# The feed-forward of the last token tile, moved into the first tiles of the next stage

## The chip, the cores and the metric

The kernel runs on one core of a Trainium2 chip. The metric is the device time of one execution in microseconds (us), taken as the median of several runs. A core has five engines that work side by side, each with an instruction queue of its own that it takes in order: TensorE (PE, matrix products, with its weight loads shown apart as PEld), VectorE (DVE), ScalarE (ACT, activation functions and copies), GpSimd (POOL) and SyncE (SP, which here issues most DMA transfers). Engines wait for one another by semaphores.

## The reference

The reference is a stack of eight residual blocks on an activation `x` of 2 sequences by 1024 tokens by 256 channels, in float32. Each block adds its output on the layernorm of `x`. Two of them follow each other at the place of the change, and a third comes after:

```
x = x + L1_attn_a(layernorm(x))   # differential attention
x = x + L1_ffn(layernorm(x))      # feed-forward
x = x + L1_attn_b(layernorm(x))   # trained linear model
x = x + L1_ffn(layernorm(x))      # the same feed-forward
```

The feed-forward works on each token by itself, with `Wg`, `Wu` and `Wd` unpacked from 4-bit codes:

```
gate = x @ Wg.T                   # 256 -> 2048
up = x @ Wu.T                     # 256 -> 2048
inter = gelu_tanh(gate) * up
out = inter @ Wd.T                # 2048 -> 256
```

The trained linear model runs through the tokens in chunks of 16, in order. For each chunk it applies a state `S` (16 by 16 for each of 16 heads) to the keys, normalizes the result, makes from it a correction `v_new`, and subtracts the product of keys and `v_new` from `S`; the queries see the state from before the chunk and the chunk's own earlier tokens. So each chunk needs the state that the chunk before left:

```
kh = ki @ S ; v_new = f(normalized kh, vi - ki)
qh = qi @ S - A @ v_new ; o = qi + ln(qh)
S = S - (ki * ei).T @ v_new
```

## The kernel before

`x` lies in on-chip memory (SBUF) for the whole run, as 16 slabs of 128 tokens. A token tile `i` (0 to 7) is slab `i` of both sequences, 256 tokens in all. A stage works through the eight tiles. Stages are set up by `build`, which runs the first four blocks, unpacks the feed-forward's weights into `deq`, and then calls `attn_d_ffn1` (differential attention and the first use of the last feed-forward) and `ttt_ffn1` (linear model and its second use).

**`attn_d_ffn1`** writes the order of its work out by hand. The attention of a tile is 16 units, and the loop runs one number `n` for each unit, with the parts of neighbouring units interleaved. Other steps are hung on a number by `add(n, step)`: those of tile `i` on the numbers of the tile after it, so that they fill gaps between attention units. They are the attention's output (`squares`, `root`, `normalize`, `project` from `attn_d_out`; the projection is L1181, its addition to `x` L1187) and then the feed-forward from `ffn1_parts`: layernorm (`stats`, `rows`, `turn`), eight gate pieces (L1255, each copied out of the one accumulator buffer `ph` by ACT at L1261), one gelu over everything (L1266), eight up pieces (L1255 again, multiplied in by DVE at L1263) and eight down pieces (L1272, added to `x` at L1279). After the last tile no attention is left to be interleaved with, and the loop runs on over the numbers that still have steps. The attention's own matmul of weights and values is `py` (L1122).

**`ttt_ffn1`** first scales the linear model's weights on DVE (`ln_w`, `ln_b`, the value part of `wt` at L1348, `wto` at L1350), which `build` loads just before through SP (L104: `wt`, `wto`, `wbeta`, `wg`) and ACT (L114: `ln_w`, `ln_b`; L1824: three small ones). These weights lie in a pool `w1`, set up after the attention's weight pool `wd` has been released (`wd_.release()`), so they take over its memory and their loads wait for its last use.

Then `ttt_inputs(0)` prepares tile 0: layernorm, transposition, projection to query, key and value, transposes of keys and queries by head, products of keys and queries (`pa`, L1416), learning rates and gates. Keys also take a way through DRAM (`uk_d`), from which they come back as `r`. The main loop then runs 8 tiles by 8 steps `n`, a step being two chunks of 16 tokens (one of each sequence). In a step PE applies the state to the queries (`pq`) and to the keys of the next step (`kh`, with a correction for the chunk just done), and makes the state's change `ds`; all these are lines L1416, 32 by 32 products in groups of 16 calls. DVE adds `ds` to `S` (L1393) and does the normalization and correction in small instructions (`ttt_step`). After these, each step runs the pieces of a list `fill[n]`: parts of the preparation of the next tile (`inputs`), of the output of the tile before (`outputs`), and of the second feed-forward of earlier tiles from `ffn1_tile`. That is cut into 14 pieces: 0 rows (layernorm), 1 turn, 2 to 9 the eight hidden chunks (gate and up into `pg` and `pu`, L1733, 16 matmul calls; gelu on ACT L1738; multiply on DVE L1739), 10 to 13 the four down pieces (L1746; the addition to `x` is L1753). A tile's pieces 0 to 4 are run in the steps 4, 6 and 7 of the tile after it (`ffn`), pieces 5 to 13 in the tile after that (`last_ffn`). In tiles 0 and 1 `last_ffn` holds empty pieces, and in tile 0 `ffn` as well. PE's order in this stage is that of the program; for the other engines a scheduler decides.

The lists that decide where a piece runs:

```
fill = [
    [outputs[0], inputs[0], *last_ffn[5:7], inputs[1]],
    [last_ffn[7], inputs[2]],
    [*last_ffn[8:10], inputs[3]],
    [last_ffn[10], inputs[7], outputs[1]],
    [last_ffn[11], outputs[2], ffn[0], inputs[4]],
    [last_ffn[12], inputs[8], inputs[5], inputs[6]],
    [last_ffn[13], ffn[1], ffn[2]],
    [ffn[3], ffn[4]],
]
```

Of the kernel before, what the change touches and what calls it, by code (L numbers as in the profile page):

```python
# [23 lines left out]
NB = T // P  # L24
# [20 lines left out]
class Net:  # L45
# [772 lines left out]
    def attn_d_ffn1(self, w, wo, cos, sin, nlam, rms_w, deq):  # L818

        nc, tc = self.nc, self.tc
        NH, NKV, D = 16, 4, 16
        with ExitStack() as ctx:
            big = ctx.enter_context(tc.tile_pool(name="d_big", bufs=1))
            work = ctx.enter_context(tc.tile_pool(name="d_work", bufs=2))
            ps = ctx.enter_context(tc.tile_pool(name="d_ps", bufs=1, space=PSUM))
            self.ps = tc.alloc_tile_pool(name="d_ps0", bufs=1, space=PSUM)  # L830
            self.small = True

            nc.vector.tensor_scalar(
                wo, wo, rms_w, 1.0 - (0.8 - 0.6 * math.exp(0.0)), ALU.mult, ALU.mult
            )

            in_g = big.tile([P, 4], F32, name="in_g")
            nc.gpsimd.memset(in_g, 1.0)
            for pattern, base, cm in (([[-32, 4]], 0, 1), ([[32, 4]], 15, -1)):
                nc.gpsimd.affine_select(  # L840
                    out=in_g, in_=in_g, compare_op=ALU.is_ge, fill=0.0, base=base,
                    pattern=pattern, channel_multiplier=cm,
                )
            half = big.tile([P, 2], F32, name="half")
            nc.vector.tensor_reduce(half[:, 0:1], in_g, AX.X, ALU.add)
            nc.vector.tensor_scalar(half[:, 1:2], half[:, 0:1], -1.0, 1.0, ALU.mult, ALU.add)

            mask = big.tile([P, T], BF16, name="mask")
            nc.gpsimd.memset(mask[:, 0 : T - P], 0.0)
            nc.gpsimd.tensor_copy(mask[:, T - P : T], self.neg)  # L850
            ctx.enter_context(self.in_order())

            kT = [big.tile([P, 2, T], F32, name=f"kT{b}") for b in range(B)]
            v = [big.tile([P, NB, NKV, 32], F32, name=f"v{b}") for b in range(B)]
            for b in range(B):
                nc.gpsimd.memset(v[b][:, :, :, D:32], 1.0)
            pools = (ps, work, w, cos, sin, half, nlam, mask)
            at, pairs = {}, []  # L860

            def add(n, *steps):
                at.setdefault(max(n, -1), []).extend(steps)

            for i in range(NB):
                n = 16 * i
                tile_ = type("tile", (), {})()
                blocks = [
                    self.attn_d_block(pools, tile_, b, i, kT[b], v[b]) for b in range(B)
                ]  # L870
                for m, step in zip(
                    (-9, -8, -6, -4, -4, -2, -2, -2, -1, -1, -1, -1, -1),
                    (*self.attn_d_inputs(ps, work, tile_, i), *blocks[0][0], *blocks[1][0]),
                ):
                    add(n + m if i else -1, step)
                for _, units in blocks:
                    pairs.extend(units)

                n += 16
                squares, root, normalize, project = self.attn_d_out(ps, work, tile_, wo, i)  # L880
                stats, rows, turn, gate, gelu, up, down = self.ffn1_parts(ps, work, i, deq)
                for m, step in (
                    (2, squares), (3, root), (4, normalize), (5, project), (5, stats), (6, rows),
                    (7, turn), *((8 + k // 2, gate[k]) for k in range(8)), (11, gelu),
                    *((13 + k // 2, up[k]) for k in range(8)),
                    *((17 + k // 2, down[k]) for k in range(8)),
                ):
                    add(n + m, step)
            nothing = type("nothing", (), {"large": False})()

            def pair(n):
                return pairs[n] if 0 <= n < len(pairs) else nothing

            def do(u, name, *args):
                f = getattr(u, name, None)
                if f:
                    f(*args)

            for step in at[-1]:
                step()  # L900
            for n in range(max(at) + 1):
                if n == 16 * 4:

                    self.ps.release()
                    self.ps = tc.alloc_tile_pool(name="d_ps1", bufs=1, space=PSUM)
                    self.small = False
                fill = at.get(n, [])
                k = (len(fill) + 2) // 3, (2 * len(fill) + 2) // 3
                u, last, turned, weighed = (pair(n - j) for j in range(4))
                do(u, "scores", 0)  # L910
                do(u, "highest", 0)
                if not u.large:
                    do(u, "exponentials")
                do(weighed, "weigh")
                do(last, "ratio")
                for step in fill[: k[0]]:
                    step()
                do(turned, "turn", 0)
                if u.large:
                    u.scores(1)  # L920
                    u.highest(1)
                for step in fill[k[0] : k[1]]:
                    step()
                do(turned, "turn", 1)
                if u.large:
                    u.exponentials()
                do(last, "difference")
                for step in fill[k[1] :]:
                    step()
            self.ps.release()  # L930
# [358 lines left out]
    def ttt_ffn1(self, w, deq):  # L1289
# [5 lines left out]

        nc, tc = self.nc, self.tc
        D = 16
        with ExitStack() as ctx:  # L1300
# [56 lines left out]
            nc.vector.memset(t.S, 0.0)  # L1357
            ctx.enter_context(tc.manual_schedule(engines={mybir.EngineType.PE}))
            data, inputs = self.ttt_inputs(0)
            for piece in inputs:  # L1360
                piece()
            vs = self.ttt_step(0, data, None)
            outputs = ffn = last_ffn = [lambda: None] * 20
            for i in range(NB):
                next_data, inputs = None, [lambda: None] * 9
                if i + 1 < NB:
                    next_data, inputs = self.ttt_inputs(i + 1)
                fill = [
# [36 lines left out]
                last_ffn, ffn = ffn, self.ffn1_tile(i, deq)  # L1405
# [357 lines left out]
def build(tc, ins, out, first=0, last=6):  # L1763
    nc = tc.nc
    with ExitStack() as ctx:
# [2 lines left out]
        net.make_constants()  # L1768
        nlam = net.diff_lambda(ins)
        todo = STAGES[first:last]  # L1770
        wd_ = tc.alloc_tile_pool(name="wd", bufs=1)
        p = "L1_attn_a_"
        wd = net.load_w(wd_, "wd", [ins[p + k] for k in ("Wq", "Wk", "Wv")])
        wdo = net.load_w(wd_, "wdo", [ins[p + "Wo_ugtd"]])
# [3 lines left out]
        with tc.tile_pool(name="w0", bufs=1) as w0:  # L1778
# [21 lines left out]
            if {"attn_d", "ttt"} & set(todo):  # L1800
                w4 = ctx.enter_context(tc.tile_pool(name="w4", bufs=1, side="right"))
                deq = [
                    net.dequantize(w4, k, ins[f"L1_ffn_{k}_packed"], ins[f"L1_ffn_{k}_scales"])
                    for k in ("gate", "up", "down")
                ]
        if "attn_d" in todo:
            net.attn_d_ffn1(wd, wdo, *rope_d, nlam, rms_w, deq)
        wd_.release()
        if "ttt" in todo:
            w1_ = ctx.enter_context(tc.tile_pool(name="w1", bufs=1))  # L1810
            p = "L1_attn_b_"
# [80 lines left out]
def program(arrays, first=0, last=6):  # L1892
    import concourse.bacc as bacc

    nc = bacc.Bacc("TRN2", target_bir_lowering=False, num_devices=1)
    ins = {
        k: nc.dram_tensor(f"in_{k}", v.shape, mybir.dt.from_np(v.dtype), kind="ExternalInput").ap()
        for k, v in arrays.items()
    }
    out = nc.dram_tensor("out", (B, T, C), F32, kind="ExternalOutput").ap()  # L1900
    with tile.TileContext(nc) as tc:
        build(tc, ins, out, first, last)
    return nc
# [9 lines left out]
```

## Time and profile before

| What | Value |
|---|---|
| Median of 3 runs | 3162.74 us (3157.12 to 3170.88) |
| The profiled execution | 3170.71 us, its span 3168.9 us |
| PE busy | 2640.7 us (83%) |
| DVE busy | 1922.1 us (61%) |
| ACT busy | 1355.2 us (43%) |
| POOL busy | 1030.5 us (33%) |
| Mean granted PE clock | 0.89 |

The page divides the span into 40 slices of 79 us. The first 29 hold roughly the blocks up to the differential attention, the last 11 the last tile's feed-forward and the linear model. The durations below are of the one profiled execution. Times of a view are counted from the start of its span. "PEclk" is the share of the full PE clock that was granted in a stretch; it is read beside each duration of a matmul, because the same matmul takes longer at a lower clock. A busy time of PE includes matmuls that run slowly, and an engine that is idle costs time only where others wait for it.

### The profile page before, as it was taken

To read this page: it belongs to the slowest core of one execution; us is meant where nothing else is said; L and a number is where in the kernel's file an instruction comes from. 1 tells how busy PE (TensorE), PEld (TensorE's weight loads), DVE (VectorE), ACT (ScalarE), POOL (GpSimd) and SP (SyncE) were. 2 spreads that over 40 slices of the span, in tenths; PEclk is the share of its full clock that TensorE was granted. 3 is DMA by queue.
4 is the path that set the end of the run, shared out by engine and by line. 5 is a ranking of instruction groups with operands and counts; after the bars stand their busy time and mean duration, and the time that the engine had idled before them with its cause. 6 is when DMAs were issued, how large, how long until landed. Compare 5 with 4: busy or idle time off the path is not lost.

```text
span 3168.9 us, 66877 instructions
## 1 busy us (share of the span) xinstructions
PE 2640.7 (83%) x26384; PEld 1622.8 (51%) x26384; DVE 1922.1 (61%) x6646; ACT 1355.2 (43%) x2713; POOL 1030.5 (33%) x1648
## 2 busy tenths in 40 slices
PE   6888889699997866978887878878867689889998
PEld 2233245343433433655655555555644567767777
DVE  4776650576765446666676867778615665665652
ACT  2785942144454334664655555656512121221210
POOL 2444210211203456566564655656500000000000
PEclk8999989799998975988989888898987699999999
DMA  3000000000001100000000000000001111001000
GB/s 111 1 1 1 1 1 0 1 1 1 1 1 27 47 8 1 1 1 1 1 1 1 1 1 1 1 1 1 1 18 22 30 23 22 10 22 36 22 10 14
DMA packets 61978, 35.38 MB, mean 11 GB/s; under 512 B 43216, under 2 KB 58080, under 8 KB 61664
## 3 DMA queue, kind: packets, MB, share of 16 engines
q1 hardware_dynamic: 59472, 29.49, 3.6%
q8 instruction: 208, 3.41, 0.4%
q10 hardware_dynamic: 2192, 1.61, 0.2%
q14 instruction: 106, 0.87, 0.1%
HBM read 22.68 MB, written 8.39 MB: 10 GB/s over the span
## 4 chain that ended last, share of the span: by engine, by line
PE 36%; DVE 13%; ACT 7%; issue 4%; POOL 3%; DMA 0%; POOLq 0%; DVEq 0%; ACTq 0%; SPq 0%
PE ph L1255 6%; PE po L1746 4%; DVE p L1057 4%; PE e L1046 4%; ACT p L1068 4%; PE pg L1733 4%; PE pu L1733 3%; PE dT L1105 3%; PE po L1272 2%; POOL p L1081 2%; DVE p L1094 2%; PE py L1122 1%; PE pa L1416 1%; PE kh L1416 1%; PE pq L1416 1%
## 5 line engine op out<-in xcount | busy, mean ns | idle before, releaser
L1057 DVE CUSTOM_DVE_ANT_0 p<-e,mask 128x512 f32<-128x512 f32 (+3 forms) x768 | 381.7, 553 | 106.4 <-PE e L1046 105.1
L1068 ACT ACTIVATE p<-p,nm 128x128 f32<-128x128 f32 (+7 forms) x512 | 389.9, 764 | 97.7 <-DVE nm L1057 88.1
L1081 POOL TENSOR_SCALAR p<-p,ra,neg_lam 128x128 f32<-128x128 f32 (+7 forms) x256 | 222.8, 870 | 235.6 <-DVE ra L1077 180.9
L1105 PE MATMUL dT<-ident,p 128*128 128x128 f32 x1152 | 200.5, 308 | 112.9 <-ACT pT L1109 29.7
L1109 ACT ACTIVATE pT<-dT 128x128 f32<-128x128 f32 (+7 forms) x256 | 165.5, 647 | 285.8 <-PE dT L1105 284.5
L1046 PE MATMUL e<-kT,qT 32*128 32x512 f32 (+3 forms) x1536 | 234.2, 625 | 28.0 <-DVE nm L1057 26.7
L196 POOL TENSOR_SCALAR ln_mv<-ln_mv 128x2 f32<-128x2 f32 x48 | 15.7, 328 | 739.9 <-DVE ln_mv L194 728.3
L1094 DVE CUSTOM_DVE_ANT_0 p<-p,rs 128x128 f32<-128x128 f32 (+7 forms) x256 | 207.8, 833 | 69.8 <-POOL p L1085 69.6
L1105 PEld LDWEIGHTS dT<-ident,p 128*128 128x128 f32 x1152 | 154.7, 158 | 173.2 <-POOL p L1085 49.5
L723 ACT ACTIVATE pr<-s 128x512 f32<-128x512 f32 (+3 forms) x384 | 157.1, 496 | 167.6 <-PE s L718 164.4
L1098 POOL TENSOR_SCALAR p<-p,md 128x128 f32<-128x128 f32 (+7 forms) x256 | 208.2, 813 | 25.4
L437 ACT ACTIVATE pr<-s 128x1024 f32<-128x1024 f32 (+1 forms) x192 | 146.1, 821 | 126.7 <-PE s L431 123.1
L1255 PE MATMUL ph<-xT,up 128*128 128x256 f32 x512 | 138.2, 419 | 20.0 <-DVE inter L1263 18.3
L683 PE MATMUL s<-kT,qT 32*128 32x512 f32 (+3 forms) x768 | 151.2, 531 | 2.3 <-ACT pr L723 1.3
L442 ACT ACTIVATE pr<-pr 128x1024 f32<-128x1024 f32 (+1 forms) x192 | 153.0, 861 | 0.0
L1255 PE MATMUL ph<-xT,gate 128*128 128x256 f32 x512 | 138.5, 417 | 15.8 <-ACT xT L225 10.8
L691 DVE CUSTOM_DVE_ANT_0 masked<-s,mask 128x128 f32<-128x128 f32 (+3 forms) x256 | 110.7, 487 | 55.0 <-PE s L683 54.6
L1746 PE MATMUL po<-down,inter 128*128 128x256 f32 x512 | 140.7, 437 | 2.2 <-DVE x L1753 1.2
L445 POOL TENSOR_SCALAR_AFFINE_SELECT pr<-pr 128x256 f32<-128x256 f32 x128 | 93.5, 747 | 146.0 <-ACT pr L442 84.4
L1733 PE MATMUL pg<-xT,gate 128*128 128x256 f32 x512 | 131.3, 401 | 7.5 <-ACT xT L225 5.5
L456 PE MATMUL py<-pr,v 128*32 128x512 f32 (+3 forms) x768 | 115.1, 541 | 26.6 <-POOL pr L445 24.6
L1255 PEld LDWEIGHTS ph<-xT,up 128*128 128x128 f32 x512 | 101.2, 207 | 62.3 <-DVE inter L1263 28.9
(301 smaller groups left out, 5440.1 us busy)
## 6 DMA issues: line engine op xcount, KB each, us to landing
uk_d<-uk SPq DMA_DIRECT2D x128, 32.0 KB, 1.8
r<-uk_d SPq DMA_DIRECT2D x8, 512.0 KB, 4.2
x<-in_L_attn_a_X SPq DMA_DIRECT2D x4, 512.0 KB, 6.1
qh_d<-qh SPq DMA_DIRECT2D x8, 256.0 KB, 2.7
o<-qh_d SPq DMA_DIRECT2D x128, 16.0 KB, 1.8
out<-x SPq DMA_DIRECT2D x4, 512.0 KB, 3.1
w<-in_L_ffn_W2T SPq DMA_DIRECT2D x1, 1024.0 KB, 7.9
pk<-in_L_ffn_gate_packed SPq DMA_DIRECT2D x8, 128.0 KB, 2.4
```

The costliest lines, as they stand in the source:

```text
L723: nc.scalar.activation(pr[:, g, off:512], tiles[g][:, 0:m], AF.Exp, scale=0.25)
L1046: nc.tensor.matmul(own.tiles[h][:, a, 0 : hi - lo], made["q"][r : r + 32, a, t, :], kT[r : r + 32, a, lo:hi], start=True, stop=True,)
L1057: nc.vector.tensor_tensor_reduce(own.p[h][a][:, lo:hi], own.tiles[h][:, a, 0 : hi - lo], neg_row[:, T - nk + lo : T - nk + hi], -1.0, 3e38 ...
L1068: nc.scalar.activation(own.p[h][a], own.p[h][a], AF.Exp, bias=own.nm[:, h, a : a + 1], scale=-1.0, accum_out=own.sm[:, h, a : a + 1],)
L1081: nc.gpsimd.tensor_scalar(p1, p1, own.ra[:, h : h + 1], nlam[:, head : head + 1], ALU.mult, ALU.mult)
L1094: nc.vector.tensor_tensor_reduce(p0, p0, p1, own.rs[:, h, 0:1], -3e38, ALU.add, ALU.max, md)
L1098: nc.gpsimd.tensor_scalar(p0, p0, md, 1.0, ALU.add, ALU.mult)
L1105: nc.tensor.transpose(dT[:, kb, :], own.p[h][0][:, kb * P : (kb + 1) * P], self.ident)
L1109: nc.scalar.activation(pT[:, 0 : qb + 1, :], dT[:, 0 : qb + 1, :], AF.Exp)
L1255: nc.tensor.matmul(ph[:, j, :], w[:, kc, m * P : (m + 1) * P], f.xT[:, kc, :], start=(kc == 0), stop=(kc == 1),)
L1733: nc.tensor.matmul(ph[:, j, :], m_[:, kc, m * P : (m + 1) * P], f.xT[:, kc, :], start=(kc == 0), stop=(kc == 1),)
L1746: nc.tensor.matmul(f.po[:, b], inter[m // 2][:, m % 2, b * P : (b + 1) * P], wd[:, m % 2, (m // 2) * C : (m // 2 + 1) * C], start=(m == 0) ...
```

## The change

The last tile's feed-forward is taken out of the loop of `attn_d_ffn1`: for `i == NB - 1` only the four output steps are hung on the numbers, and `ffn1_parts` isn't called. Instead `ttt_ffn1` makes it with `ffn1_tile(NB - 1, deq)` (`owed`), in the 14 pieces of the second form. Pieces 0 to 4 (layernorm, turn, three hidden chunks) are run between the parts of `ttt_inputs(0)`; pieces 5 to 9 (five hidden chunks) fill the empty places of `last_ffn` in tile 0, at steps 0, 1, 2, 4 and 6; pieces 10 to 13 (down) fill those of tile 1, at steps 2, 4, 5 and 6. The linear model needs `x` of the last tile only when it prepares tile 7, in tile 6. The pool `wd` is no longer released before the linear model's weights are set up.

```
@@ attn_d_ffn1
                 squares, root, normalize, project = self.attn_d_out(ps, work, tile_, wo, i)
+                if i == NB - 1:
+
+                    for m, step in enumerate((squares, root, normalize, project)):
+                        add(n + 2 + m, step)
+                    continue
                 stats, rows, turn, gate, gelu, up, down = self.ffn1_parts(ps, work, i, deq)
@@ ttt_ffn1
             data, inputs = self.ttt_inputs(0)
-            for piece in inputs:
+            owed = self.ffn1_tile(NB - 1, deq)
+            begin, turn, keys, targets, diagonals, ag01, ag23, low_ranks, rates = inputs
+            for piece in (
+                begin, turn, keys, owed[0], targets, owed[1], diagonals, owed[2], ag01, owed[3],
+                ag23, low_ranks, owed[4], rates,
+            ):
                 piece()
             vs = self.ttt_step(0, data, None)
             outputs = ffn = last_ffn = [lambda: None] * 20
+            nothing = [lambda: None]
+            owed_by_tile = [
+                nothing * 5 + [
+                    owed[5], *nothing, owed[6], *nothing, owed[7], *nothing, owed[8], *nothing,
+                    owed[9],
+                ],
+                nothing * 8 + [*nothing, owed[10], *nothing, *owed[11:14]],
+            ]
             for i in range(NB):
                 next_data, inputs = None, [lambda: None] * 9
+                if i < 2:
+                    last_ffn = owed_by_tile[i]
@@ build
-        wd_ = tc.alloc_tile_pool(name="wd", bufs=1)
+        wd_ = ctx.enter_context(tc.tile_pool(name="wd", bufs=1))
...
             net.attn_d_ffn1(wd, wdo, *rope_d, nlam, rms_w, deq)
-        wd_.release()
```

## The prediction

> **What bounds the kernel now.** I read in this order: the page's chain of waits, the timeline around the end of the differential attention, the busy times by stage, and those by step of the trained linear model. The chain gives TensorE (PE) 36% and names both feed-forward matmul lines, L1255 (6%) and L1733, among its largest parts. The timeline of the last tile's feed-forward (start, length, engine, line, operation; in brackets the idle time before it and what ended it):
>
> ```profile
> 2283.87 1.94 PE L1122 MATMUL py<-pT,v 128*32 128x128 f32 x58 [0.82 <-ACT pT L1109]
> ...
> 2301.89 0.42 DVE L1187 TENSOR_TENSOR x<-x,po 128x256 f32<-128x256 f32 x1 [1.22 <-PE po L1181]
> ...
> 2315.74 3.77 PE L1255 MATMUL ph<-xT,gate 128*128 128x256 f32 x8 [0.68 <-ACT inter L1261]
> ...
> 2320.18 1.99 PE L1255 MATMUL ph<-xT,gate 128*128 128x256 f32 x8 [0.68 <-ACT inter L1261]
> ...
> 2380.38 0.42 DVE L1279 TENSOR_TENSOR x<-x,po 128x256 f32<-128x256 f32 x1 [7.34 <-PE po L1272]
> ```
>
> The attention's last work, its addition to x, ends at 2302.3; the feed-forward's ends at 2380.8. Between them one buffer `ph` makes PE, ScalarE (ACT) and VectorE (DVE) take turns, and beside it run only the loads and scalings of the next stage's weights. The busy times by stage (stretch and length, busy time with instructions of PE, weight load, DVE, ACT and POOL, granted PE clock, DMA share, GB/s):
>
> ```profile
> 2302.30:2380.70 78.40, 55.04 (x196) 40.06 (x196) 11.01 (x32) 10.19 (x11) 1.28 (x3) 0.85 0.06 18
> 2380.70:2413.70 33.00, 22.34 (x307) 13.71 (x307) 14.79 (x63) 8.79 (x20) 3.87 (x9) 0.74 0.14 33
> ...
> 2421.00:2482.80 61.80, 41.62 (x1556) 30.34 (x1552) 37.55 (x193) 11.62 (x30) 1.40 (x2) 0.67 0.12 27
> 2482.80:2553.40 70.60, 56.46 (x1644) 41.28 (x1636) 49.96 (x249) 15.60 (x37) 3.93 (x8) 0.76 0.11 25
> ...
> 2649.20:2737.70 88.50, 77.93 (x1770) 62.58 (x1760) 55.10 (x257) 18.35 (x42) 3.89 (x8) 0.96 0.09 21
> ```
>
> The rows are the exposed feed-forward, the preparation of the linear model's tile 0, its tile 0, tile 1 and tile 3. Tile 3 carries a whole feed-forward and is PE-bound (77.93 busy of 88.50). Tile 0 carries none: PE is idle for 20 us and has 0.67 of its clock. Tile 1 carries three of eight hidden chunks and idles for 14. So there is room, but not all of it is usable, since a chunk also delays what stands behind it on PE.
>
> Hence the steps, each from one state addition (L1393) to the next: tile 0 steps 0 and 1, tile 1 steps 5 and 6, tile 3 steps 5 and 6.
>
> ```profile
> 2420.99:2426.10 5.11, 3.54 (x168) 2.99 (x164) 3.62 (x22) 0.82 (x2) 0.00 (x0) 0.50 0.01 3
> 2426.10:2434.45 8.35, 8.19 (x197) 4.38 (x190) 4.52 (x25) 1.81 (x6) 0.00 (x0) 0.65 0.01 2
> ...
> 2527.09:2538.39 11.30, 10.14 (x425) 8.92 (x425) 7.53 (x33) 2.21 (x6) 3.55 (x6) 0.70 0.02 5
> 2538.39:2544.24 5.85, 5.16 (x118) 4.28 (x115) 4.22 (x23) 1.19 (x2) 0.00 (x0) 1.00 0.02 6
> ...
> 2700.39:2716.00 15.61, 10.91 (x430) 9.25 (x434) 8.87 (x29) 2.20 (x6) 2.94 (x5) 0.98 0.01 3
> 2716.00:2728.48 12.48, 11.79 (x154) 9.63 (x149) 4.66 (x22) 1.19 (x2) 0.00 (x0) 0.75 0.00 1
> ```
>
> Where little is asked of PE (step 0), the clock is 0.50; tile 1's step 6, which has a hidden chunk, takes 5.85 us at 1.00.
>
> [...] the same eight matmuls take 3.77 us and then 1.99, and sparse tile 0 has a clock of 0.67 where dense tile 3 has 0.96. [...]
>
> **The change part by part.**
> 1. Removed: the stretch from 2302.3 to 2380.8, 78.5 us, with its table load of 1.28. The built instruction order has no L1255 matmul of the last tile left. It has one table load at the first moved gelu, behind the copies that release the recurrence's products; those products run on PE meanwhile, so I count nothing, 1.3 us without that cover.
> 2. Weights of the linear model. They get memory of their own and wait for the last `py` matmul (ends 2285.8), where they waited for the last output projection (2301.9). The same six SP and five ACT issues go 16 us earlier. But DVE's scalings of them stand in its queue before the additions of tile 6's feed-forward and the attention's last normalization. `ln_b` took 5.6 us to land, its scaling 0.4: issued at 2286.3 it holds DVE until 2292.4, while the addition that lets 7.2 us of `po` matmuls start was free at 2289.5. Cost 3.3 us (bounds 0 and 8; at 8 a late `wto` also holds DVE).
> 3. Preparation of tile 0 (33.0 us): three hidden chunks and a layernorm more. A chunk is 16 matmuls; dense ones near the end of the run start 3.45 us apart (rows at 3125.41 and 3128.86), so 6.9 at half rate. Chunk 0 lies between the transposes of k and q and the products that wait for their copy, which covers 1.4 us (2402.3 to 2403.7); chunks 1 and 2 stand bare before matmuls that are due. Full rate 3 x 3.45 - 1.4 = 9.0, half rate 19.3. The layernorm's 13 small DVE instructions interleave with three such chains: 1 us. At the stage's clock of 0.74 I take 13 (10 to 20).
> 4. Tile 0: one chunk each in steps 0, 1, 2, 4, 6. A step's lower bound is its PE time at full clock (busy times clock) plus 3.5, or its old length if longer; the upper is the same work at half rate plus 6.9. Step 0: 5.3 to 10.4; step 1: 8.8 to 17.5; step 2 (7.70 long, PE 4.85, clock 1.00): 8.4 to 16.6; step 4 (7.18, PE 4.22, 0.62): 7.2 to 12.1; step 6 (5.07, PE 1.27, 0.68): 5.9, tile 1's, to 8.6. Denser work lifts the clock, so I take values in the lower half, nearest to full where the clock was high: 7.5, 10.5, 9.2, 9.2, 6.9. Growth 2.4 + 2.2 + 1.5 + 2.0 + 1.8, less 1 for the clock of steps 3, 5, 7: 9 us. Each chunk's multiply (0.69) stands in DVE's queue before the next step's variance, which waits for products behind the same chunk.
> 5. Tile 1: four down pieces of 16 matmuls (3.6 us, half of a 7.17 row) in steps 2, 4, 5, 6. Step 2 (16.20, PE idle 7.8, DVE busy 14.2): 0.5. Steps 4 and 5 then hold what tile 3's hold: 10.63 - 8.52 = 2.1 and 15.61 - 11.30 = 4.3. Step 6: tile 3's 12.48 ran at 0.75, at full rate 5.2 + 3.6 = 8.8; taken 10.9, so 5.0. Sum 12.
> 6. SP's and POOL's queues: no DMA more; two POOL normalizations (1.1 us each) lie under the 5.6 us of query and key projection. Nothing; 2 us without that cover.
>
> Sum: -78.5 + 3.3 + 13 + 9 + 12 = -41 us against the profiled execution's 3170.71 (span 3168.9), so 3129.5. That execution is 8 us above the median; on the median of 3162.74 I predict 3122.
>
> **Rivals.**
> - The gaps swallow nearly all, since denser PE work also raises the clock of what was there. For: clocks of 1.00 in tile 1's steps 6 and 7, which have chunks. Against: two chunks of the preparation stand bare. Preparation 9, weights 1.5, tile 0 1.5, tile 1 6: growth 18, gain 60, 3102.
> - Partly cold: about half of the pieces start at half rate, growth midway between 37 and the 89 below: 63, gain 15, 3147. For: the clock drops even in dense stretches (0.75 in tile 3's step 6). Against: that tile's 0.96.
> - Slower: the clock stays at half through preparation and both tiles. The moved work then costs 3.3 + 20.3 + 32 + 34 = 89 us by the upper bounds (tile 1's from the same formula), and steps that got nothing (3 and 5 of tile 0; 1, 3 and 7 of tile 1) 16.6 more: 106 against 78.5, so 3190. It decides once the mean clock there falls below about 0.6. For: 0.50 in step 0 of both tiles. [...]
> - That the change does not do what it says, the instruction order excludes.
>
> **How the numbers follow.** Forecast 0.70, swallowed 0.15, partly cold 0.11, slower 0.04. The range 3101 to 3144 takes in the bounds of parts 2 to 5 short of the cold cases. Half a per cent, 16 us, is about what a measurement can tell; beyond it lie the forecast, the swallowed case and half of the partly cold one: faster 0.91, same 0.06, slower 0.03.
>
> **What would show it.** Right: L1255-type matmuls of seven tiles only; the first `kh` about 62 us earlier (78.5 less 3.3 and 13); tile 0 near 71 us and tile 1 near 83; clocks above 0.67 and 0.76; tiles 2 to 7 as before. Wrong: a DVE wait for weights above 8 us, preparation above 55 us, or a clock near 0.5 in tile 0.

## The result, and the profile after

The changed kernel takes 3127.9 us (median of 4 runs, 3120.82 to 3129.27) where the kernel before took 3166.81 beside it; the ratio is 0.9871, with a 95% interval of 0.9850 to 0.9893, so 34 to 47 us. Two more measurements of it gave 0.9848 (0.9822 to 0.9874) and 0.9872 (0.9851 to 0.9894). The prediction was 3122, a gain of 41 on a kernel before of 3162.74, which is a ratio of 0.9871. Line numbers from here on are those of the kernel after or of its variants, unless a view is said to be of before; they are higher by 5 to 21 (the down piece L1272 is L1277 there, the recurrence L1416 is L1437).

Two profiled executions with spans of 3168.9 and 3127.5 us divide the difference as follows. The cuts are the end of the last `py` matmul, the end of the attention's last addition to `x`, the end of the feed-forward's, and the state additions that begin tiles 0, 1 and 2.

| Stretch | before | after | difference | predicted |
|---|---|---|---|---|
| start to `py` | 2285.8 | 2284.6 | -1.2 | 0 |
| `py` to the attention's last addition | 16.5 | 24.1 | +7.6 | +3.3 |
| last tile's feed-forward | 78.5 | - | -78.5 | -78.5 |
| to the first state addition | 40.2 | 49.9 | +9.7 | +13 |
| tile 0 | 61.8 | 70.5 | +8.7 | +9 |
| tile 1 | 70.6 | 82.8 | +12.2 | +12 |
| tile 2 to the end | 615.5 | 615.5 | 0 | 0 |

The zero in the last row is closer than such a stretch can be known: two more profiles of the changed kernel have 618.3 and 615.3 there, and those of the other experiments, whose work from tile 2 on is the same, lie between 607.6 and 626.6.

The busy times by stage of the kernel after, in the columns known from the prediction: `py` to the attention's last addition, preparation, tile 0, tile 1, tile 2.

```profile
2284.64:2308.76 24.12, 17.19 (x56) 12.75 (x56) 9.69 (x35) 0.00 (x0) 2.05 (x5) 0.77 0.20 58
2308.76:2358.70 49.94, 36.38 (x548) 24.99 (x548) 23.44 (x102) 13.39 (x28) 6.50 (x14) 0.77 0.10 22
2358.70:2429.20 70.50, 57.49 (x1636) 44.92 (x1632) 40.55 (x198) 14.36 (x35) 1.36 (x2) 0.84 0.10 23
2429.20:2512.00 82.80, 68.50 (x1708) 51.29 (x1700) 54.77 (x252) 15.48 (x37) 3.89 (x8) 0.85 0.11 23
2512.00:2607.30 95.30, 83.62 (x1770) 66.66 (x1760) 55.22 (x257) 18.46 (x42) 3.89 (x8) 0.89 0.09 19
```

The first two stretches of the kernel before, for comparison (the second from the feed-forward's end to the first state addition):

```profile
2285.81:2302.31 16.50, 13.08 (x56) 10.23 (x56) 8.05 (x27) 0.00 (x0) 2.05 (x5) 1.00 0.00 1
...
2380.80:2421.00 40.20, 24.97 (x496) 16.13 (x496) 20.30 (x87) 9.72 (x23) 5.23 (x11) 0.71 0.12 28
```

The first row of each is the interesting pair. The same 56 PE matmuls are busy for 17.19 us instead of 13.08, at a clock of 0.77 instead of 1.00: not only was there a wait, the work itself became slower. The chain of waits of the kernel after (start, length, what it is) shows where:

```profile
2285.08 6.42 DMA ln_b<-in_L_attn_b_ln_b
2292.32 9.84 PE po L1277 x32
```

and the timeline gives DVE's wait and what it did to PE (the last line is of the kernel before):

```profile
2291.52 0.41 DVE L1351 TENSOR_TENSOR wb<-ln_w,ln_b 1x256 f32<-1x256 f32 x1 [3.37 <-DMA ln_b<-in_L_attn_b_ln_b]
...
2292.32 9.82 PE L1277 MATMUL po<-down,inter 128*128 128x256 f32 x32 [4.03 <-DVE x L1284]
...
2289.97 7.17 PE L1272 MATMUL po<-down,inter 128*128 128x256 f32 x32 [0.51 <-DVE x L1279]
```

DVE stood for 3.37 us at the scaling that needs `ln_b`. Behind it in its queue was the addition that releases the buffer `po`, so PE idled for 4.03 us. The 32 matmuls after that took 9.82 us; in the kernel before the same 32 took 7.17. (The trace has two records for each float32 matmul call: nine calls of the same shape, added in an experiment below, show as x18. The x32 here are 16 calls, and a hidden chunk, which the section on the kernel before gives 16 calls, has 8, in 16 records.) The clock granted in this execution is 1.00 from the end of `py` (2284.64) to 2290.89, in the middle of the idle time, and 0.50 from there to 2297.72.

The steps of tile 0 (chunks in steps 0, 1, 2, 4 and 6):

```profile
2358.69:2366.18 7.49, 7.49 (x196) 6.31 (x188) 4.28 (x22) 1.42 (x3) 0.00 (x0) 0.74 0.01 2
2366.18:2379.05 12.87, 10.52 (x197) 7.25 (x187) 5.29 (x25) 2.40 (x7) 0.00 (x0) 0.87 0.00 1
2379.05:2387.35 8.30, 8.30 (x188) 6.17 (x188) 7.23 (x37) 1.92 (x5) 0.00 (x0) 1.00 0.02 5
2387.35:2392.52 5.17, 3.57 (x150) 2.11 (x140) 3.77 (x23) 0.96 (x3) 0.00 (x0) 1.00 0.28 48
2392.52:2403.13 10.61, 8.60 (x215) 7.02 (x215) 5.14 (x25) 3.85 (x8) 1.26 (x2) 0.84 0.33 81
2403.13:2414.53 11.40, 10.10 (x425) 8.92 (x424) 6.50 (x29) 2.20 (x6) 0.10 (x1) 0.70 0.02 4
2414.53:2422.58 8.05, 6.26 (x115) 4.89 (x111) 4.23 (x23) 0.60 (x1) 0.00 (x0) 0.79 0.01 2
2422.58:2429.19 6.61, 2.64 (x204) 2.25 (x196) 4.10 (x23) 1.01 (x3) 0.00 (x0) 0.87 0.19 54
```

Steps 5 and 7 of tile 0 in the kernel before:

```profile
2454.48:2467.73 13.25, 11.12 (x452) 9.73 (x444) 6.59 (x29) 2.21 (x6) 0.00 (x0) 0.69 0.02 4
...
2472.80:2482.78 9.98, 3.27 (x207) 2.93 (x203) 4.50 (x22) 1.04 (x3) 1.40 (x2) 0.50 0.35 99
```

The steps with a chunk grew by 2.4, 4.5, 0.6, 3.4 and 3.0 us, 13.9 together. Steps 5 and 7, which got nothing, became 1.9 and 3.4 us shorter. The clock of the tile rose from 0.67 to 0.84.

Most of what step 7 lost is not the clock's doing. In the kernel before, DVE waits in it for `r`, the next tile's keys on their way back from DRAM. The first three lines are of before, the last two of after:

```profile
2473.84 0.34 SPq L1667 DMA_DIRECT2D qh_d<-qh  x1
2474.75 0.34 SPq L1515 DMA_DIRECT2D r<-uk_d  x1
2479.50 0.24 DVE L1643 TENSOR_TENSOR gp<-gp,r 128x64 f32<-128x64 f32 x1 [2.55 <-DMA r<-uk_d]
...
2398.57 0.34 SPq L1536 DMA_DIRECT2D r<-uk_d  x1
2423.48 0.34 SPq L1688 DMA_DIRECT2D qh_d<-qh  x1
```

In before, the load of `r` stands in SP's queue behind a transfer (`qh_d`) that needs the tile's last query products. In after it stands ahead of it and is issued 24 us before step 7 begins, and DVE doesn't wait for it. So the order in SP's queue, which a scheduler decides, changed with the moved pieces. The profiles of the experiments bear this out: in all eleven with the pieces `r` is issued early, and in the three without them (before, the weight edit alone, the pieces left out) 2 us into step 7.

### The profile page after: what moved, and what is told of

It reads as the page before. It is cut to its first block, busy times and chain, and to the rows that moved or that the text cites. A ratio compares the mean times of both kernels' runs of the same rounds, so it can differ in the third digit from the quotient of the medians.

```text
span 3127.5 us, 66883 instructions
## 1 busy us (share of the span) xinstructions
PE 2628.4 (84%) x26384; PEld 1618.6 (52%) x26384; DVE 1923.2 (61%) x6646; ACT 1351.5 (43%) x2712; POOL 1031.1 (33%) x1648
## 4 chain that ended last, share of the span: by engine, by line
PE 36%; DVE 13%; ACT 7%; issue 4%; POOL 3%; DMA 0%; POOLq 0%; ACTq 0%; DVEq 0%
PE ph L1260 5%; PE po L1767 4%; PE pg L1754 4%; DVE p L1062 4%; PE pu L1754 4%; PE e L1051 4%; ACT p L1073 4%; PE dT L1110 3%; POOL p L1086 2%; DVE p L1099 2%; PE po L1277 2%; PE py L1127 1%; PE pq L1437 1%; PE kh L1437 1%; PE pa L1437 1%
## 5 line engine op out<-in xcount | busy, mean ns | idle before, releaser
L1754 PE MATMUL pg<-xT,gate 128*128 128x256 f32 x576 | 154.6, 415 | 11.0 <-issue 5.5
L1767 PE MATMUL po<-down,inter 128*128 128x256 f32 x576 | 156.8, 434 | 3.2 <-issue 2.0
L1754 PE MATMUL pu<-xT,up 128*128 128x256 f32 x576 | 142.2, 391 | 0.0
L1767 PEld LDWEIGHTS po<-down,inter 128*128 128x128 f32 x576 | 123.5, 219 | 25.8 <-issue 2.8
L1760 DVE TENSOR_TENSOR inter<-inter,pu 128x512 f32<-128x512 f32 x72 | 49.3, 685 | 142.1 <-PE pu L1754 142.1
```

The costliest lines, as they stand in the source:

```text
L1754: nc.tensor.matmul(ph[:, j, :], m_[:, kc, m * P : (m + 1) * P], f.xT[:, kc, :], start=(kc == 0), stop=(kc == 1),)
L1767: nc.tensor.matmul(f.po[:, b], inter[m // 2][:, m % 2, b * P : (b + 1) * P], wd[:, m % 2, (m // 2) * C : (m // 2 + 1) * C], start=(m == 0) ...
```

## The experiments

Theory A is that of the prediction, with one addition from the first profile: a moved piece costs what PE lacks in the step that it lands in, and a PE that idles loses its clock and pays for it in the work that follows. Ratios below are to the kernel before, measured beside it on the same chip. Whole runs of one kernel differ by up to 30 us, while a median of four has an interval of some 7 us either way, so small effects are read from the stages.

**The changed kernel beside its variants.** It was run again beside two groups of the variants. Beside the kernels with the weight edit, those with other places of the chunks alone, and the last repeat it wasn't, so these are compared with it through their ratios to before.

> The changed kernel again, beside the three that follow, as what they are compared with. Every theory: 0.987 of the time of before, about 3128 us.

Measured 0.9848, the median 3125.16. Its profile has 23.5 us from `py` to the last addition, 47.7 of preparation, 72.8 and 83.5 for tiles 0 and 1.

> The changed kernel once more, beside the next two. Every theory: 0.985 to 0.987 of the time of before.

Measured 0.9872, 3132.35; 23.4, 47.8, 72.6 and 83.8 us. Over the three profiles these four stretches grew by 38.2 to 38.5 us in all, counted from the one profile of before. They are far steadier than the whole run: the end of `py`, before which nothing was changed in the work, lies between 2273.9 and 2290.0.

**The wait for `ln_b` alone.**

```
+        ln_b = net.load_row(wd_, "ln_b", ins["L1_attn_b_ln_b"])
...
-                "ln_b": net.load_row(w1_, "ln_b", ins[p + "ln_b"]),
+                "ln_b": ln_b,
```

> The changed kernel with ln_b loaded at the start of the run, so that DVE doesn't wait for it at the end of the attention. Theory A (the wait of 3.4 us lets PE idle for 4 us, and the idle PE then works at half clock): the time from the end of py to the last addition of the attention falls from 24.1 us to about 17, the last 32 po records from 9.8 us to about 7.2, and the whole run by about 7 us. Theory B (only the wait counts, the half clock after it is the clock's own swing): 3.4 us, po stays near 9.8.

The stretch fell to 17.4 us. The timeline of PE in this kernel:

```profile
2288.00 7.17 PE L1277 MATMUL po<-down,inter 128*128 128x256 f32 x32 [1.41 <-DVE x L1284]
2297.10 1.13 PE L1186 MATMUL po<-wdo,yT 128*128 128x256 f32 x4 [1.93 <-DVE yT L1178]
2298.75 1.13 PE L1186 MATMUL po<-wdo,yT 128*128 128x256 f32 x4 [0.51 <-DVE x L1192]
```

PE waits for 1.41 us instead of 4.03, and the 32 matmuls take 7.17 us. Of the 6.7 us gained, 2.6 are wait and 4.1 are matmuls that ran at full rate: theory A. The whole run didn't show it: 0.9848, the same ratio as that of the changed kernel beside it. In this profile 3 of the 7 us are left at the end of tile 2 (319.8 us from `py` against 322.6 and 323.2), since tile 1 took 86.2, and none at the end of the run (842.9 us from `py` against 842.8 in the first profile). One profile can't say whether that is given back or the clock's swing.

**A busy PE in place of an idle one**, with DVE's wait left as it is:

```
+                if i == NB - 2 and b == 0:
+                    idle = ps.tile([P, 512], F32, tag="py", name="idle")
+                    for m in range(9):
+                        nc.tensor.matmul(
+                            idle[:, 0:C], f.inter[:, m, 0:P], wd[:, m % 2, 0:C],
+                            start=True, stop=True,
+                        )
```

> The changed kernel with nine matmul calls more (18 records, about 4 us at full clock, their result is read by nothing) in PE's idle time before the last down pieces of tile 6. DVE's wait for ln_b stays. Theory A (the idle PE loses its clock): po falls from 9.8 us to about 7.2 and the two output projections from 1.65 and 2.07 to 1.13 each, the whole run by 3 to 4 us although work was added. Theory B (the clock's own swing): po stays near 9.8, the run is as long as the changed kernel or 0.5 us longer.

```profile
2287.06 4.05 PE L1288 MATMUL idle<-down,inter 128*128 128x256 f32 x18
2290.94 7.07 PE L1277 MATMUL po<-down,inter 128*128 128x256 f32 x32
2299.94 2.00 PE L1186 MATMUL po<-wdo,yT 128*128 128x256 f32 x4 [1.93 <-DVE yT L1178]
2302.46 2.07 PE L1186 MATMUL po<-wdo,yT 128*128 128x256 f32 x4 [0.51 <-DVE x L1192]
```

With useless work in the gap the 32 matmuls take 7.07 us; in the three profiles of the changed kernel, with waits of 4.03, 3.39 and 3.28 us, they took 9.82, 10.18 and 10.19. That tells the two theories apart: it is the idleness that costs the clock. The profiles of all the experiments agree. In the seven in which PE waits there for 2.8 to 4.0 us, the 32 matmuls take 8.75 to 10.19 us. In the seven in which it waits for at most 1.4 us, or has filler work, they take 7.07 to 7.17. The second half of the expectation missed. The projections took 2.00 and 2.07 us, behind 1.93 us of idle PE, where the run with `ln_b` early has 1.13 us each behind the same 1.93; what made the difference is not shown. The stretch is 21.4 us, the whole run 0.9853: no difference that can be told.

**The moved work taken away.** The 14 pieces are empty, so the last tile's first feed-forward is left out.

```
-            owed = self.ffn1_tile(NB - 1, deq)
+            owed = [lambda: None] * 14
```

> The changed kernel without the last tile's first feed-forward: the 14 pieces do nothing, so that part of the computation is left out. Theory A (the moved work costs what the two traces show: preparation 9.7, tile 0 8.7, tile 1 12.2): 31 us less than the changed kernel, tile 0 back near 62 us and tile 1 near 71. Rival C (the gaps swallow it, and the longer tiles come from the clock or from the schedule): at most 10 us less, tiles 0 and 1 stay above 67 and 78. Rival D (without the chunks PE is colder and tile 0 slower than in before): under 25 us less.

Measured 0.9768 (0.9746 to 0.9790), 3099.27 us, 26 below the changed kernel beside it. Preparation took 39.5 us and tile 0 59.4, as expected; tile 1 76.1 instead of 71, and tile 2 102.5 instead of 95. Rival C (swallowed) falls: the medians lie 26 us apart where it allowed 10, the slowest run without the pieces (3102.86) is 15 us below the fastest with them (3117.69), and tiles 0 and 1 didn't stay above 67 and 78. A's 31 us lie inside what the two intervals leave, but tile 1 speaks for a part of D: without the pieces its clock is 0.71, and tile 2's 0.85. The kernel with the weight edit alone, below, has the same pieces in tile 1 as before and took 76.1 us there too, at a clock of 0.67. So the 12 us of tile 1 are the upper end of its cost; against these two profiles it is 7 or 8.

**The weight edit, taken out and taken alone.**

```
-        wd_ = ctx.enter_context(tc.tile_pool(name="wd", bufs=1))
+        wd_ = tc.alloc_tile_pool(name="wd", bufs=1)
...
             net.attn_d_ffn1(wd, wdo, *rope_d, nlam, rms_w, deq)
+        wd_.release()
```

> The changed kernel with the attention's weight pool released as before, so that only the feed-forward moves and the loads wait for the last output projection. Theory A (the weight edit moves a stall of DVE from the layernorm of tile 0 to the attention's end, and is worth little): py to the last addition back at 16.5 us (24.1 and 23.5 in the changed kernel), from there to the first state addition about 53 (49.9 and 47.7); together some 3 us shorter than the changed kernel, not to be told from it in the whole run. Rival E (the memory of their own is needed, the loads of 10 us are otherwise bare): first state addition 5 us or more later than in the changed kernel, measured from py.

```profile
2290.95 7.17 PE L1277 MATMUL po<-down,inter 128*128 128x256 f32 x32 [0.51 <-DVE x L1284]
...
2313.34 1.23 PE L220 MATMUL ln_t<-ident,ln_xn 128*128 128x128 f32 x4 [10.50 <-POOL ln_xn L205]
```

The stall has moved: `po` no longer waits, and the transposes of tile 0 wait for 10.50 us instead of 5.38. 16.5 and 54.1 us make 70.6 from `py` to the first state addition, against 74.0, 71.2 and 71.2. The run is at 0.9842 (0.9824 to 0.9859), not to be told from the changed kernel. Rival E falls; the edit of the pool contributes nothing that shows.

The other way round, the kernel before with only

```
-        wd_ = tc.alloc_tile_pool(name="wd", bufs=1)
+        wd_ = ctx.enter_context(tc.tile_pool(name="wd", bufs=1))
...
-        wd_.release()
```

> The kernel before with the weight pool kept, that is the weight edit alone, without the move. Theory A: py to the last addition of the attention 23 to 24 us instead of 16.5, DVE's stalls of 4 us in the layernorm of the feed-forward gone, so the stretch up to the last addition of the feed-forward 3 us longer than in before; whole run within half a per cent of before. Rival E (earlier loads are a gain): this stretch 3 us shorter or more.

23.9 us to the attention's last addition and 115.2 to the first state addition, 4 us more than before's 135.2 together; ratio 1.0009 (0.9996 to 1.0022). That is as theory A had it. With the ratio of 0.9842 for the move alone, the gain is the feed-forward's move; the weight edit adds none that shows.

**Where the chunks of tile 0 stand.** Spread to steps 0, 3, 4, 6 and 7:

```
-                    owed[5], *nothing, owed[6], *nothing, owed[7], *nothing, owed[8], *nothing,
-                    owed[9],
+                    owed[5], *nothing, *nothing, *nothing, *nothing, owed[6], owed[7], *nothing,
+                    owed[8], owed[9],
...
-                    [ffn[3], ffn[4]],
+                    [last_ffn[14], ffn[3], ffn[4]],
```

> The changed kernel with the five chunks of tile 0 in steps 0, 3, 4, 6 and 7, where PE has least to do, instead of 0, 1, 2, 4 and 6. Theory A (a chunk costs what PE lacks in its step): step 1 back near 8.4 us, step 2 near 7.7, step 3 up to 7 to 8.5, step 7 to 8.5 to 10; tile 0 67 to 72 us (70.5 and 72.8 in the changed kernel's two profiles), whole run the same within half a per cent. Rival C (the room is one for the whole tile): tile 0 as in the changed kernel.

The other lists got an empty place at their end. Steps 3 and 7 of tile 0:

```profile
2379.92:2388.48 8.56, 8.49 (x194) 6.15 (x186) 4.44 (x23) 1.56 (x4) 0.00 (x0) 0.83 0.32 54
...
2416.68:2423.56 6.88, 5.86 (x232) 4.94 (x220) 4.58 (x25) 1.61 (x4) 0.00 (x0) 1.00 0.19 53
```

Step 3 pays 3.4 us, a whole chunk, although PE was idle for 1.6 of its 5.17 us in the changed kernel; in before it was full (5.15 of 5.15), at a clock of 0.67. Step 7, where PE was busy for 2.64 of 6.61 in the changed kernel, pays 0.3. So theory A met the sum better than the steps: step 3 came out just above its range, step 7 below its range, and step 1 at 9.7 instead of 8.4. Tile 0 takes 68.5 us. That alone tells nothing, since six profiles with the chunks of tile 0 in their first places (the changed kernel's three, those of the two experiments on the wait, and the one with the pool released) have 67.7 to 73.3 there. The whole run is at 0.9859: the same.

And all five bunched in step 5:

```
-                nothing * 5 + [
-                    owed[5], *nothing, owed[6], *nothing, owed[7], *nothing, owed[8], *nothing,
-                    owed[9],
-                ],
+                nothing * 12 + [lambda: [piece() for piece in owed[5:10]], *nothing],
```

> The changed kernel with all five chunks of tile 0 in step 5. Theory A (a chunk costs what PE lacks in its step; five of 3.45 us bare are 17): step 5 about 28 to 31 us instead of 11.4, the other steps as in before (5.1, 8.4, 7.7, 5.2, 7.2, -, 5.1, 10.0), tile 0 about 78 us, 6 to 8 more than the changed kernel. Rival C (what counts is the room in the whole tile): tile 0 at 70 to 73.

```profile
2386.03:2391.82 5.79, 3.87 (x151) 2.96 (x146) 4.31 (x24) 3.37 (x7) 0.00 (x0) 0.64 0.34 60
2391.82:2423.12 31.30, 28.19 (x517) 24.16 (x513) 11.12 (x35) 5.19 (x11) 1.40 (x2) 0.88 0.04 16
2423.12:2428.09 4.97, 1.67 (x112) 1.49 (x106) 3.62 (x22) 0.00 (x0) 0.00 (x0) 0.50 0.02 3
```

Step 5 takes 31.3 us, and the steps beside it are as long as in the kernel without the pieces, 5.8 and 5.0 us. Tile 0 takes 75.5 us, 2.8 to 5 more than in the changed kernel, where 6 to 8 were expected (step 7 stayed at 7.3), and more than in any of those six profiles. The run is at 0.9884 (0.9867 to 0.9901), against 0.9848 to 0.9872. Its four runs (3130.9 to 3136.6 us) all lie above the four of the spread kernel beside it (3122.7 to 3129.0). The place in the tile counts, not the room in all of it.

**Both edits together**, `ln_b` early and the chunks spread:

> The changed kernel with both edits: ln_b loaded at the start, and the five chunks of tile 0 in steps 0, 3, 4, 6 and 7. Theory A: py to the last addition about 17 us, tile 0 at 67 to 71, the whole run some 8 us (a quarter of a per cent) below the changed kernel of this call. Rival F (what is gained at the attention's end is given back later in the stage by the clock, as the whole run of the first edit alone hints): py to the first state addition shorter by 6 to 8 us, but py to the end of tile 2 the same within 3 us.

Measured 0.9831 (0.9806 to 0.9855), 3117.12 us, beside 3132.35 for the changed kernel; 17.0 us to the last addition, tile 0 at 65.7, a little below its range, and 309.4 us from `py` to the end of tile 2 against 322.4. Rival F falls for this kernel.

> The kernel with ln_b early and the chunks of tile 0 respread, once more. If the two edits are worth the 10 us that the stages show, the ratio to before is again below 0.985 (0.9831 the first time; the changed kernel had 0.9871, 0.9848 and 0.9872). If the first time was luck of the clock, it is 0.985 to 0.987.

0.9836 (0.9813 to 0.9858), with 16.9 us, 66.0 and 309.4. So this version beats the changed kernel: the mean of its two ratios is 0.3% (10 us) below that of the changed kernel's three. The intervals of single measurements still touch, but where the two ran side by side, all four runs of this version (3108.9 to 3124.4 us) lie below all four of the changed kernel (3125.6 to 3134.8). The stages agree: 13 us less at the end of tile 2, twice alike. A lead there need not last, since the kernel with nine filler calls also stood at 312.7 and then ended no earlier than the changed kernel (846.1 us from `py` to the end of the run). This version took 828.9 and 831.9 from `py` to the end, the changed kernel 842.8 to 845.8. How much each of the two edits gives isn't shown; neither alone could be told from the changed kernel.

Last, the same with PE kept busy by eleven unread matmul calls after the attention's last projection:

> The same with eleven matmul calls (22 records, about 4.9 us at full clock, read by nothing) on the idle PE after the attention's last projection, where it waits 5.3 us for the layernorm of tile 0. Theory A (idle PE loses its clock, and pays in the work that follows): the query and key projection falls from 6.6 us toward 4.7, the preparation from 48 to 50 us to about 46, the whole run 2 to 4 us below the kernel without them. Theory B (the clock swings by itself): projection and preparation as without.

```profile
2295.81 4.91 PE L1196 MATMUL idle<-wdo,yT 128*128 128x256 f32 x22
...
2300.81 0.75 DVE L193 BATCH_NORM_STATS2 ln_st<-x 128x6 f32<-128x256 f32 x2 [4.38 <-PE idle L1196]
```

The preparation and the whole run should have become shorter, and didn't. This run says nothing of the clock, though. The filler added a wait: the layernorm's statistics now wait 4.38 us for its last matmul, so the preparation grew to 54.1 us, and the idle gap that it was to fill lay behind it again (5.07 us). The ratio is 0.9842.

## Why the prediction was right

1. The removed stretch: 78.5 us, gone as a whole, and the feed-forward's return in later stages was priced. That the rest of the run shows no difference at all is luck, as said above. The page has 2712 ACT instructions instead of 2713 and the same 26384 matmuls: the work was moved, not saved.
2. The weights: the wait was named, and the term mis-sized, 3.3 us against 7.6 (7.0 and 6.9 in the other two profiles). The recorded figures give 2.9 rather than 3.3 (2292.4 less 2289.5); measured, the 32 matmuls began 3.5 us later after `py` than in before, since `ln_b` took 6.4 us to land instead of 5.6. What failed is the assumption that the 7.2 us of `po` matmuls behind it cost 7.2 us as before. PE lost its clock in the gap, and 4.1 us followed in these matmuls and the projections; the two experiments on this wait showed it. The prediction had reckoned with a lower clock for the chunks and forgotten it for the idle PE that it had itself found.
3. The preparation: 9.7 us (7.6 in two more profiles) against 13, and below the stated bound of 10. Only the first chunk ran in part at half rate (5.2 us); the other two took 3.7 each, and the products `pa` behind them 3.8 us instead of 5.9. The table load was hidden, as said: it ends before the first `pg` does.
4. Tile 0: 8.7 us (11.0 and 10.8) against 9. That the sum was met is luck, for two larger errors cancel. The steps with a chunk grew by 13.9 us where 9.9 were counted: step 1 took 12.9 us instead of 10.5 and step 4 10.6 instead of 9.2. The untouched steps 5 and 7 gave back 5.2 us where 1 was set for the clock of three steps. About half of that is DVE's wait of 2.55 us for `r`, gone with the new order of SP's queue, for which part 6 had counted nothing.
5. Tile 1: 12.2 us (12.9 and 13.2) against 12. Steps 4, 5 and 6 took 10.64, 15.10 and 10.97 us where 10.63, 15.61 and 10.9 had been read off a tile that holds the same pieces. These were the best-founded estimates, and the best met. Step 2 grew by 2.1 us instead of 0.5, and step 1 gave back 1.1. That the growth fits so well rests on before's one profile with 70.6 us; two others without the down pieces have 76.1.
6. The first `kh` came 61.5 us earlier, predicted 62. The error of +4.3 in part 2 and of -3.3 in part 3 cancel in this number, and 1.2 us of it were there before the end of `py`; it is not as good as it looks.

Of the rivals, the swallowed case is excluded by the run without the pieces. The cold case didn't come about: the clock of tiles 0 and 1 is 0.80 to 0.85 in the three profiles. The growth of the four stretches was 38 us, predicted 37. The moved pieces alone were priced at 34 of these; the stages give 31 and their removal 26. So the mechanism, a long stretch taken out and paid back by less than half in later ones, is shown, while the closeness of the total owes something to errors that cancel.

## What to carry to other kernels

Price a moved piece step by step, against the idle time that the bounding engine has in the very step that it enters, and best from a step elsewhere in the trace that already holds the same pieces. A wait that leaves TensorE idle for some microseconds can be paid twice, once as the wait and once as matmuls at half rate after it, so count both: here waits of 2.8 to 4.0 us were followed by 1.6 to 4.1 us of slower matmuls. A load that is issued earlier gains nothing if an instruction that needs it stands earlier in an in-order queue than the work that others wait for: here DVE stood for 3.37 us at the scaling with `ln_b`, PE for 4.03 us behind it, and the weight edit alone gave a ratio of 1.0009. And where a scheduler orders the queues, compare every engine's order before and after a change: a load that moved ahead in SP's queue took away a wait of 2.55 us that nobody had set out to remove.

## What the runs showed of the hardware

- The same idle time didn't always cost the clock. After PE had been idle for 1.93 us the first output projection took 2.00 us in the run with nine filler calls, and 1.13 us in the run with `ln_b` early. So the length of the idle time alone doesn't tell; what else counts is not shown.
- Tile by tile the granted clock rose with the share of time in which PE was busy: 0.67 with 41.62 of 61.80 us (tile 0 of before), 0.84 with 57.49 of 70.50 (tile 0 of after), 0.96 with 77.93 of 88.50 (tile 3 of before). It doesn't follow from that share alone: tile 1 of before has 0.76 with 56.46 of 70.60 us, the last tile's feed-forward there 0.85 with 55.04 of 78.40.
- PE was partly busy and stayed at half clock in step 0 of tile 0 in before: 3.54 of 5.11 us, 1.11 of them with four transposes (128 by 128) and the rest with 32 by 32 products, at 0.50. With one chunk (128 by 128) in it, in after, PE is busy for all of the step's 7.49 us and the clock is 0.74. Whether the size of the products has a part in it was not tried.
- Work added to a step can shorten its neighbours: steps 5 and 7 of tile 0 lost 1.9 and 3.4 us, and the clock is only a part of it. Step 7 of the bunched kernel ran at 0.50 as in before and took 7.30 us instead of 9.98; the 2.7 us are about DVE's wait of 2.55 us for `r`, which it doesn't have. Step 5 became shorter at nearly the same clock (0.69 and 0.70); why stays open.
